# Masked attention on one Trainium2 core: the opening batch reordered, one tie dropped, four sums moved to VectorE

## The chip, the cores and the metric

The kernel runs on one core of a Trainium2 chip. The metric is device time in microseconds (us) of one execution. A core has the engines TensorE (PE in the profile; its weight loads are PEld), VectorE (DVE), ScalarE (ACT), GpSimd (POOL) and SyncE (SP); each works through its own queue of instructions in order, and engines wait for one another through semaphores. SP's queue issues most of the transfers (DMA), POOL's the gathers and scatters by index. Matrix products land in PSUM, a memory of eight banks of 512 float32 columns on 128 partitions; all else is in SBUF.

## The reference

Sixteen batches; each is a matrix x of 512 features by 1024 tokens with a mask of 0 and 1 over the tokens. Queries, keys and values are all the same projection.

```python
q = xt @ Wq.T                                   # xt: tokens by features, 1024 x 512
qh = q.reshape(B, T, NH, dk).transpose(0, 2, 1, 3)          # 8 heads of 64
scores = scale * jnp.einsum('bhqd,bhkd->bhqk', qh, qh)
logits = (scores * cmask + (1.0 - cmask) * NEG) * rmask
attn = jax.nn.softmax(logits, axis=-1)
ctx = jnp.einsum('bhqk,bhkd->bhqd', attn, qh)
out = ctx.transpose(0, 2, 1, 3).reshape(B, T, D) @ Wo.T
x = x + jnp.transpose(out, (0, 2, 1))
```

A masked key gets no weight. The row of a masked query has only equal logits, so it gets the plain mean over all tokens.

## The kernel before

Only tokens with mask 1 need attention: about half of 1024. For each batch the kernel gathers these (512 to 544 rows, `A`) and works on them alone; the masked tokens get one common row, made from the mean of x over all tokens. That mean needs the sum of every feature of x over 1024 tokens, which is read from a second copy of x, feature by feature: four transfers of 128x1024 (`load_all`, tile xm, two buffers) and four sums (`sum_half`, L459, on ScalarE). Batch 0 takes another way (`load_half`). Products are kept exact by splitting a float32 factor into two float16 parts, high and low, and summing three products.

The work of a batch b, and which lines do it:

- the gather (L422 on POOL) brings 128 rows of x at a time (tile xa; the rest in xt); the index comes from `index` (eight small matmuls L333, read by VectorE at L336)
- `xt` transposes each 128 rows on TensorE (L519, four matmuls into a tile pm); ScalarE writes the high part xh (L477), VectorE the low part xl (L478)
- `query(b, e, g)`: half g of the columns of feature chunk e, twelve matmuls (L548), copied by ScalarE (L552); after g=1 VectorE multiplies the edge (L555) and `qsplit` makes high and low parts (hl, L571 to L573), which four transfers of SP (L582 to L585) spread into xx, where the two heads of chunk e stand in forms of 128 and of 64 partitions
- `value(b, e)` turns the queries into rows (L608 for batch 0, L611 later; copied at L615) and sums squares of each row per head (sd, L594 or L598, then L599)
- `peaks`, `top`, `bottom` find for four heads the largest square, which bounds every score: `peaks` reduces on VectorE (smcol, L662 and L665), `top` transposes on TensorE (L671) and takes the maximum on VectorE (m, L674), `bottom` brings it to all partitions on TensorE (L681) and VectorE writes the exponentials' bias nm (L684 to L687)
- `scores(b, p, u)`: for head pair p and the query blocks 2u and 2u+1, eight or more matmuls (L774) into the tile pss, then four exponentials on ScalarE (L789) with their sums
- `attend(b, p)`: 16 products of exponentials and values (L809, each shown as two matmuls), copied by ScalarE (L832); `tail_scores` and `attend_tail` (L720, L827) for the columns past 512
- `recip_sums` and `recip_rows` invert the sums of the exponentials (L847 to L868, with a transpose L863 and two transfers), `norm` multiplies (L915 to L923), `project` multiplies with Wo (L933), adds x (L939) and scatters the rows (L1002)

pss has six banks. The scores of one call take banks 0 to 3, with A=544 a part of bank 4; the attention takes parts of banks 4 and 5; the start of bank 5 is the `spot` where index, `top` and `bottom` put their small results while the loop runs. Accesses of different engines to pss are ordered by the framework as one tile, and where they are in different banks the kernel lifts that order with `other_banks`. pm, the tile of all other products, has two buffers.

Every batch is a loop over 18 steps: head pair p by block i, with two steps in between that hold no block. Scores are made at steps 0, 3, 5, 7, 9, 12, 14 and 16; attention of a pair follows the first scores of the next. A dictionary `plan`, written out by hand, says for (step, half) what of the previous batch (o), of this one (b) and of the next one (n) stands where; half 0 comes after the step's scores and before its attention, half 1 after it. Batch 0 has a `plan` of its own. From batch 0 on TensorE's order is exactly that of the program (`manual_schedule`). The order on VectorE, ScalarE and the queues is made by a scheduler from priorities (`high_priority`) and due times.

`self.left` holds the exponentials of the last scores, `self.spot_reads` the reads of the spot. `self.exp` is the last exponential; `behind` asks the scheduler to put an instruction after others, `last_hl` is the latest copy of `qsplit`.

Of the kernel before, what the change touches and what calls it, by code (L numbers as in the profile page):

```python
# [15 lines left out]
ALU = mybir.AluOpType  # L16
AX = mybir.AxisListType
# [30 lines left out]
class Fast:  # L48
# [407 lines left out]
    def sum_half(self, b, k):  # L456
        s = self.st[b]
        with self.behind(*self.exp):
            self.nc.scalar.activation(s["xm"][k], s["xm"][k], AF.Copy, accum_out=s["ms2"][:, k:k + 1])  # L459

    def load_all(self, b, c, after=None):

        if c == 0:
            self.source(b)
        t = self.sb([P, T], F32, "xm", 2)
        src = self.x_nat[bass.ds(self.st[b]["row"], 1), c * P:(c + 1) * P, :].rearrange("o p t -> (o p) t")
        self.once(self.nc.sync.dma_start(out=t, in_=src), after)
        self.st[b]["xm"].append(t)
# [198 lines left out]
    def top(self, b, g):  # L667

        nc, s = self.nc, self.st[b]
        pt = self.spot(P)  # L670
        self.spotted(nc.tensor.transpose(pt, self.smcol[g], self.ident))  # L671
        m = s["m"] = self.sb([P, 1], F32, "m", 2)
        with self.tc.high_priority(offset=HPO):
            self.spot_reads += [nc.vector.tensor_reduce(m, pt, AX.X, ALU.max).ins] * self.spots  # L674

    def bottom(self, b, g):

# [64 lines left out]
    def scores(self, b, p, u):  # L742


        nc, s = self.nc, self.st[b]
        A = s["A"]
        if "z" not in s:
            s["z"] = self.sb([P, H, 4], F32, "z", 2)
            s["zt"] = self.sb([P, 2], F32, "zt", 2)
        xx = s["xx"][p]  # L750
        flat = self.ps.rearrange("p k n -> p (k n)")
        first = FIRST[A]
        places = [(k, 2 * u + i, first + (2 * k + i) * A) for k in range(2) for i in range(2)]
        last = []
        out = self.context_out

        calls, lanes = [], ([], [])
        for j, (k, i, at) in enumerate(places):
            rows = slice(i * P, (i + 1) * P)
            h = xx[k * DK:(k + 1) * DK, 3 * k, :]  # L760
            cuts = [at] + [c for c in (512 * (j + 1),) if at < c < at + A] + [at + A]
            for c0, c1 in zip(cuts, cuts[1:]):
                cols = slice(c0 - at, c1 - at)
                calls.append((c0, c1, xx[:, 2 * k, rows], xx[:, 2 * k + 1, cols]))
                if j == 1 and c0 == 1024:
                    calls.append((c0, c1, xx[:, 2 * k, rows], xx[:, 2 * k, cols]))
                else:
                    lanes[k].append((c0, c1, h[:, rows], h[:, cols]))
        for j in range(max(map(len, lanes))):
            calls += [l[j] for l in lanes if j < len(l)]  # L770
        banks = [c[0] // 512 for c in calls]
        for n, (c0, c1, w, x) in enumerate(calls):
            with self.behind(*last), self.tc.high_priority(offset=HPO if n else 0):
                m = nc.tensor.matmul(flat[:, c0:c1], lhsT=w, rhs=x, start=banks[n] not in banks[:n], stop=banks[n] not in banks[n + 1:])  # L774
            if out and banks[n] < 4:
                self.other_banks(m.ins, out)
            elif out and banks[n] not in banks[:n]:
                self.needs(m.ins, out)
            self.other_banks(m.ins, *self.spot_reads)
            if n == 0 and self.left:  # L780
                self.needs(m.ins, *self.left)
            last = [m.ins]
        self.beat = last[0]
        self.left, self.context_out = [], None
        ps = {}
        for j in (3, 0, 1, 2):
            k, i, at = places[j]
            t = self.sb([P, C], F32, "p", 12)[:, :A]
            e = nc.scalar.activation(t, flat[:, at:at + A], AF.Exp, bias=s["nm"][p // 2][:, p % 2 * 2 + k:p % 2 * 2 + k + 1],  # L789
                                     scale=SCALE, accum_out=s["z"][:, 2 * p + k, i:i + 1]).ins  # L790
            self.exp = [e]
            self.left.append(e)
            ps[k, i] = t
        s.setdefault("p", {}).setdefault(p, {}).update(ps)
# [250 lines left out]
    def run(self, flag):  # L1045
        B = self.B
        L = lambda f, *a: lambda: f(*a)
# [8 lines left out]
        def query(n, e, g):  # L1056
            u = [(1.37, L(self.query, n, e, g))]
            return u + [(0, L(self.qsplit, n, e))] if g else u

        def value(n, e):  # L1060
            return [(0.45, L(self.value, n, e))]
# [11 lines left out]
        for b in range(2, B):  # L1073
            n = 1 if b < B - 3 else 2 if b == B - 3 else 1 if b == B - 2 else len(queue)
# [96 lines left out]
        if True:  # L1171
            stack = ExitStack()
            for b in range(B + 1):
                o, n = b - 1, b + 1
# [6 lines left out]
                free, sums, rows, third, tail, rest = {}, [], [], [], [], []  # L1181
# [13 lines left out]
                pk, tp, bt = ((lambda o, g, f=f, c=c: [(c, L(f, o, g))]) for f, c in ((self.peaks, 0), (self.top, 0.1), (self.bottom, 0.1)))  # L1195
                new = [g for g in groups if b == g[0] - 2], [g for g in groups if b == g[0] - 1]
                if n < B:
                    q, x, v = (lambda e, g: query(n, e, g)), xt(n), (lambda e: [(0.25, L(self.value, n, e))])
                    tc, tv = ((lambda g, f=f, c=c: [(c, L(f, n, g))]) for f, c in ((self.tail_copy, 0), (self.value_tail, 0.25)))
                    rng = [(0, L(self.range_x, n, c)) for c in range(DC)]  # L1200
# [5 lines left out]
                    if b:  # L1206
                        pre = [(0, L(f, *g)) for g in new[0] for f in (self.permute, self.active)]
                        post = [(0.3, L(self.slots, *g)) for g in new[0]] + [(0, L(self.facts_sums, *g)) for g in new[1]]
                        end = [(0.1, L(self.facts_end, *g)) for g in new[1]]
                        plan = {(0, 0): sums + x[:2], (0, 1): x[2:4],  # L1210
                                (3, 0): rows + x[4:] + q(0, 0) + second, (3, 1): pre + q(0, 1) + carry, (4, 0): value(b, 3),
                                (5, 1): vt(b, 1) + pk(b, 1), (6, 0): post,
                                (7, 0): third + q(1, 0) + tp(b, 1), (7, 1): q(1, 1) + P_(0) + bt(b, 1), (8, 0): tc(0) + v(0) + end + rng[:2],
                                (10, 0): tv(0) + tail + q(2, 0), (11, 0): hot + rng[2:] + early,
                                (12, 0): q(2, 1), (12, 1): index + P_(1) + v(1), (13, 0): take[:3],
                                (14, 1): rest + pk(n, 0), (16, 0): P_(2) + take[3:], (16, 1): q(3, 0) + tp(n, 0) + q(3, 1),
                                (17, 0): bt(n, 0) + v(2) + tc(1) + [(0, L(self.means, n))]}
                        carry = P_(3)
                    else:
                        pre = [(0, L(f, *g)) for g in new[0] for f in (self.permute, self.active)]  # L1220
                        post = [(0.3, L(self.slots, *g)) for g in new[0]]
                        rng0 = [(0, apart(self.range_x, 0, c)) for c in range(DC)]
                        plan = {(0, 0): g1[4:] + query(0, 3, 0) + value(0, 2) + rng0,
                                (3, 0): query(0, 3, 1) + x[:1] + value(0, 3) + pk(b, 1), (4, 0): x[1:2],
                                (5, 0): x[2:3], (5, 1): x[3:],
                                (7, 0): tp(b, 1) + q(0, 0) + bt(b, 1) + q(0, 1), (8, 1): pre + q(1, 0),
                                (9, 1): post, (11, 0): hot + q(1, 1),
                                (12, 0): tc(0) + v(0) + rng[:2] + q(2, 0), (13, 1): index,
                                (14, 0): tv(0) + q(2, 1) + rng[2:] + take[:3], (14, 1): v(1) + q(3, 0) + pk(n, 0),
                                (16, 0): q(3, 1) + tp(n, 0) + take[3:], (16, 1): bt(n, 0),  # L1230
                                (17, 0): v(2) + tc(1) + [(0, L(self.means, n))]}
                else:
# [18 lines left out]
                for k, x in enumerate([x for x in (b + 2, self.extra.get(b + 2)) if x is not None and x < B]):  # L1251
                    if x > b + 2:
                        self.start(x)
                    elif b + 2 in self.extra.values():
                        continue
                    for c in range(DC):
                        at = 3 * c + k + (0 if b else 4)
                        free.setdefault(at, []).append(L(self.load_all, x, c, None if b else first_top))
                        free.setdefault(at + (2 if b + 2 in self.extra else 4), []).append(L(self.sum_half, x, c))
                def fill(st, half):  # L1260
                    for _, f in plan.get((st, half), []):
                        f()
# [175 lines left out]
```

## Time and profile before

| | |
|---|---|
| time, three runs | 974.54, 974.04, 973.05 us; median 974.04 |
| the profiled execution | 971.93 us, of which its span 970.2 us |
| granted TensorE clock, mean | 0.999 |
| chain of waits that ended last: share of PE, DVE, DMA, ACT | 80%, 7%, 5%, 3% |
| exponentials L789, 512 | 703 ns each, and 206 ns for reading their sum |
| scores L774, 1856 matmuls | 213.0 us |
| queries L548, three lines of 512 matmuls | 141.8, 141.1, 140.9 us |
| sums L459 of 128x1024, 60 | 1071 ns each |
| maximum L674, 32 | 290 ns each; VectorE idle before them 9.8 us for L789, 0.5 us for a product |
| transfers xm, 60 | 512 KB each |

Lines are those of the kernel before. An idle time is put down to the event that ended it. The span is that of the profiled execution; times of instructions are from its start. In the lists of work by order of time each line has the start, how long the group lasted, engine, line, operation, tiles and shape, the number of instructions, and in brackets how long the engine was idle before and for whom. Matmuls overlap: the list shows one of 512 columns as 0.38 us, while the next starts 0.22 us later.

### The profile page before, as it was taken

The numbers are of one execution on the slowest core, as the hardware profiler recorded it, in microseconds if no ns is written. First come the engines' busy times: TensorE is split into PE (matmuls) and PEld (weight loads), VectorE is DVE, ScalarE is ACT, GpSimd is POOL, SyncE is SP. The second block draws the span as 40 slices with busy tenths as digits, with TensorE's granted clock in tenths as the row PEclk, the third lists the DMA queues.
The fourth block names the chain that finished last, engine by engine and source line by source line (L and its number), as shares of the span: only waits on it lengthen the run. The fifth ranks groups of instructions, "written<-read, shape, count | busy, mean of one in ns | idle before, by whom it ended". The sixth has DMA issues, their size and how long they took to land.

```text
span 970.2 us, 22817 instructions
## 1 busy us (share of the span) xinstructions
PE 932.3 (96%) x8124; PEld 580.9 (60%) x8124; DVE 717.7 (74%) x2439; ACT 650.3 (67%) x1677; POOL 305.5 (31%) x309
## 2 busy tenths in 40 slices
PE   7788999999999999999999999999999999999997
PEld 4555666666666666666666566666666656565543
DVE  7768778777677767887688777877877778785664
ACT  5678857666777675776767678665767766565651
POOL 3101023043250522415144150422515135243452
PEclk9999999999999999999999999999999999999999
DMA  7656556466665676756657777654757757555552
GB/s 220 176 154 194 147 168 178 140 189 203 177 197 145 195 199 216 204 147 201 181 177 212 205 234 216 179 164 135 205 159 243 226 153 212 143 163 162 170 179 102
DMA packets 78568, 176.30 MB, mean 182 GB/s; under 512 B 14480, under 2 KB 22416, under 8 KB 78448
## 3 DMA queue, kind: packets, MB, share of 16 engines
q1 hardware_dynamic: 57392, 107.09, 39.2%
q0 software_dynamic: 21056, 67.68, 22.4%
q8 instruction: 66, 1.08, 0.5%
q14 instruction: 54, 0.44, 0.2%
HBM read 91.36 MB, written 33.91 MB: 129 GB/s over the span
## 4 chain that ended last, share of the span: by engine, by line
PE 80%; DVE 7%; DMA 5%; issue 3%; ACT 3%; SPq 1%; POOL 1%; POOLq 0%; DVEq 0%; ACTq 0%
PE pss L809 21%; PE pss L774 17%; PE pm L933 16%; PE pm L548 15%; PE pss L827 2%; PE pm L519 2%; DMA xm<-x_nat_in 2%; DMA xa<-x_in,idx 2%; PE pss L720 1%; PE pm L611 1%; ACT p L789 1%; DVE xl L478 1%; PE pss L933 1%; DVE xa L939 1%; DMA xx<-hl 1%
## 5 line engine op out<-in xcount | busy, mean ns | idle before, releaser
L789 ACT ACTIVATE p<-pss,nm 128x528 f32<-128x528 f32 (+2 forms) x512 | 354.5, 703 | 103.6 <-PE pss L774 101.5
L809 PE MATMUL pss<-p,v 128*64 128x264 f32 (+2 forms) x2048 | 242.4, 389 | 0.0
L774 PE MATMUL pss<-xx 128*128 128x118 f16 (+17 forms) x1856 | 213.0, 287 | 6.0 <-ACT p L789 3.8
L1002 POOL DMA_INDIRECT y_out<-xa,idx x68 | 81.8, 1203 | 409.5 <-DVE nq L686 98.3
L809 PEld LDWEIGHTS pss<-p,v 128*64 128x64 f32 x2048 | 141.4, 137 | 85.9 <-issue 4.8
L774 PEld LDWEIGHTS <-xx 128*128 128x128 f16 (+1 forms) x1856 | 103.2, 96 | 86.4 <-issue 34.3
L548 PE MATMUL pm<-xh,wqh 128*128 128x264 f16 (+5 forms) x512 | 141.8, 277 | 3.2 <-DVE xl L478 1.3
L548 PE MATMUL pm<-xh,wql 128*128 128x264 f16 (+5 forms) x512 | 141.1, 275 | 0.0
L548 PE MATMUL pm<-xl,wqh 128*128 128x264 f16 (+5 forms) x512 | 140.9, 275 | 0.0
L548 PEld LDWEIGHTS <-wqh 128*128 128x128 f16 x1024 | 96.4, 97 | 31.0 <-issue 11.9
L422 POOL DMA_INDIRECT xa<-x_in,idx x68 | 73.5, 1080 | 126.2 <-DMA y_out<-xa,idx 46.4
L789 ACT ACTIVATION_READ_ACCUMULATOR p<-pss,nm 128x1 f32 x512 | 105.4, 206 | 0.0
L933 PE MATMUL pm<-woh,ch 128*128 128x512 f16 x240 | 91.1, 380 | 0.0
L933 PE MATMUL pm<-woh,cl 128*128 128x512 f16 x240 | 90.9, 379 | 0.0
L933 PE MATMUL pm<-wol,ch 128*128 128x512 f16 x240 | 90.9, 379 | 0.0
L552 ACT ACTIVATE q<-pm 128x264 f32<-128x264 f32 (+5 forms) x128 | 51.0, 398 | 45.1 <-PE pm L548 44.9
L615 ACT COPY v<-pm 128x512 f32<-128x512 f32 x64 | 37.5, 587 | 57.9 <-PE pm L611 56.2
L939 DVE SCALAR_TENSOR_TENSOR xa<-pm,xa 128x512 f32<-128x512 f32 x61 | 41.7, 683 | 45.8 <-PE pm L933 45.3
L1002 POOL DMA_INDIRECT y_out<-xi,idx x60 | 64.1, 1068 | 34.3 <-PE pss L720 14.5
L933 PEld LDWEIGHTS <-ch 128*128 128x128 f16 x480 | 44.8, 98 | 47.5 <-issue 4.1
L422 POOL DMA_INDIRECT xi<-x_in,idx x60 | 59.9, 999 | 22.1 <-issue 15.8
L459 ACT ACTIVATE xm<-xm 128x1024 f32<-128x1024 f32 x60 | 64.1, 1071 | 2.0 <-DMA xm<-x_nat_in 1.9
(228 smaller groups left out, 1464.0 us busy)
## 6 DMA issues: line engine op xcount, KB each, us to landing
xm<-x_nat_in SPq DMA_DIRECT2D x60, 512.0 KB
xx<-hl SPq DMA_DIRECT2D x208, 136.0 KB
rb<-rd SPq DMA_DIRECT2D x72, 132.0 KB
xx<-hl SPq DMA_DIRECT2D x48, 128.0 KB
pt<-c SPq DMA_DIRECT2D x36, 132.0 KB
pt<-p SPq DMA_DIRECT2D x36, 132.0 KB
rb<-rd SPq DMA_DIRECT2D x32, 136.0 KB
ub<-ud SPq DMA_DIRECT2D x16, 256.0 KB
```

Of the source, the lines that this page charges most:

```text
L422: dma = self.nc.gpsimd.indirect_dma_start(out=tile[:n], out_offset=None, in_=self.x, in_offset=bass.IndirectOffsetOnAxis(ap=idx, axis=0))
L459: self.nc.scalar.activation(s["xm"][k], s["xm"][k], AF.Copy, accum_out=s["ms2"][:, k:k + 1])
L519: self.pe = nc.tensor.transpose(pt[:, c, :], x[:n, c * P:(c + 1) * P], self.ident[:n, :n]).ins
L548: self.beat = nc.tensor.matmul(pq, lhsT=w[:, c, e * P:(e + 1) * P], rhs=xx[:, c, cols], start=(k == 0), stop=(k == 3 * DC - 1)).ins
L552: nc.scalar.activation(s["q"][:, e, cols], pq, AF.Copy, scale=1.0 / (SX * SW))
L615: nc.scalar.copy(v, pv)
L774: m = nc.tensor.matmul(flat[:, c0:c1], lhsT=w, rhs=x, start=banks[n] not in banks[:n], stop=banks[n] not in banks[n + 1:])
L789: e = nc.scalar.activation(t, flat[:, at:at + A], AF.Exp, bias=s["nm"][p // 2][:, p % 2 * 2 + k:p % 2 * 2 + k + 1], scale=SCALE, accum_out ...
L809: mm = nc.tensor.matmul(pav[k * DK:(k + 1) * DK, g], lhsT=s["v"][p][:, i, k * DK:(k + 1) * DK], rhs=ps[k, i][:, cols], start=(i == 3), sto ...
L933: mm = nc.tensor.matmul(po[:cols.stop - cols.start], lhsT=a[:, e, cols], rhs=w[:, e, :], start=(e == 0 and k == 0), stop=(e == DC - 1 and ...
L939: return self.nc.vector.scalar_tensor_tensor(x, po, 1.0 / (SX * SW), x, ALU.mult, ALU.add).ins
L1002: dma = self.nc.gpsimd.indirect_dma_start(out=self.out, out_offset=bass.IndirectOffsetOnAxis(ap=idx, axis=0), in_=x, in_offset=None)
```

## The change

1. `top`: the maximum is told (`other_banks`) that it has nothing to do with the exponentials in `self.left`. The reading of `bottom`'s result (L684) keeps its order as it was.
2. `scores`: for the first call (batch 0, pair 0, blocks 0 and 1) the eight matmuls are sorted by head: the four that fill banks 0 and 1 first, then the four of banks 2 and 3; the four exponentials are issued in the order of the banks and not the last first.
3. The plan of batch 0: the transpose of chunk 1 of batch 1 moves from step 4 to step 5, behind that step's scores, beside chunk 2; query (2,1) of batch 1 moves from step 14, behind its scores, to step 13, behind `index`. `index` moves from the second half of step 13 to its first.
4. `sum_all`: the four sums of batch 1 become reductions on VectorE, put behind the latest `qsplit`. Batch 2's four sums, in the same stretch, stay on ScalarE; so do those of all later batches.

```diff
+    def sum_all(self, b, c, other):
+        s = self.st[b]
+        if not other:
+            return self.sum_half(b, c)
+        with self.behind(self.last_hl), self.nc.allow_low_precision(reason="float32"):
+            self.nc.vector.tensor_reduce(s["ms2"][:, c:c + 1], s["xm"][c], AX.X, ALU.add)
...
         with self.tc.high_priority(offset=HPO):
-            self.spot_reads += [nc.vector.tensor_reduce(m, pt, AX.X, ALU.max).ins] * self.spots
+            i = nc.vector.tensor_reduce(m, pt, AX.X, ALU.max).ins
+        if self.spots:
+            self.other_banks(i, *self.left)
+            self.spot_reads.append(i)
...
+        opening = b == 0 and p == 0 and u == 0
+        if opening:
+            calls.sort(key=lambda c: c[0] // (2 * A))
...
-        for j in (3, 0, 1, 2):
+        for j in (0, 1, 2, 3) if opening else (3, 0, 1, 2):
...
-                                (3, 0): query(0, 3, 1) + x[:1] + value(0, 3) + pk(b, 1), (4, 0): x[1:2],
-                                (5, 0): x[2:3], (5, 1): x[3:],
+                                (3, 0): query(0, 3, 1) + x[:1] + value(0, 3) + pk(b, 1),
+                                (5, 0): x[1:3], (5, 1): x[3:],
                                 (7, 0): tp(b, 1) + q(0, 0) + bt(b, 1) + q(0, 1), (8, 1): pre + q(1, 0),
                                 (9, 1): post, (11, 0): hot + q(1, 1),
-                                (12, 0): tc(0) + v(0) + rng[:2] + q(2, 0), (13, 1): index,
-                                (14, 0): tv(0) + q(2, 1) + rng[2:] + take[:3], (14, 1): v(1) + q(3, 0) + pk(n, 0),
+                                (12, 0): tc(0) + v(0) + rng[:2] + q(2, 0), (13, 0): index + q(2, 1),
+                                (14, 0): tv(0) + rng[2:] + take[:3], (14, 1): v(1) + q(3, 0) + pk(n, 0),
...
-                        free.setdefault(at + (2 if b + 2 in self.extra else 4), []).append(L(self.sum_half, x, c))
+                        free.setdefault(at + (2 if b + 2 in self.extra else 4), []).append(L(self.sum_all, x, c, b == 0 and x == 1))
```

In `plan`, `x` is `xt` of the next batch by chunks, `q(e, g)` its `query`, `v(e)` its `value`, `tp`, `bt` and `pk` are `top`, `bottom` and `peaks`, `tc` and `tv` the tail's copy and value, `take` the gathers of the batch after it, `hot`, `pre` and `post` the preparation of its index.

## The prediction

> **What bounds the kernel now.** I read the page's busy shares first, then the engines' busy time by stretches, then TensorE's and VectorE's work in order of time in the one stretch where TensorE is not full, and last the built programs' order of instructions and waits, which says what a wait is for but holds no time.
>
> ```profile
> PE 932.3 (96%) x8124; PEld 580.9 (60%) x8124; DVE 717.7 (74%) x2439; ACT 650.3 (67%) x1677; POOL 305.5 (31%) x309
> ```
>
> TensorE (PE) is the bound: only 970.2 - 932.3 = 37.9 us of the span are without a matmul. By stretches (us; then busy us and instructions of each engine, granted clock, DMA share, GB/s):
>
> ```profile
> 30.00:40.00 10.00, 6.47 (x45) 3.39 (x43) 7.92 (x26) 6.59 (x21) 2.78 (x3) 1.00 1.02 262
> 50.00:60.00 10.00, 7.04 (x55) 4.61 (x52) 5.52 (x22) 7.43 (x20) 0.00 (x0) 1.00 0.51 141
> 70.00:80.00 10.00, 8.25 (x80) 5.41 (x80) 9.19 (x35) 9.93 (x27) 1.89 (x2) 1.00 0.69 205
> 80.00:90.00 10.00, 7.88 (x77) 4.95 (x74) 8.39 (x32) 6.72 (x18) 2.77 (x3) 1.00 0.80 258
> 300.00:400.00 100.00, 98.93 (x896) 63.29 (x894) 73.68 (x243) 70.36 (x182) 35.34 (x34) 1.00 0.65 191
> ```
>
> The reader is to see that the holes lie in batch 0 (30 to 90 us), and that a later stretch is 99% full. Whatever batch 0 saves should therefore reach the end, and edits to other batches have next to nothing to win. TensorE's holes there, and the first line shown is the scores' wait for a transfer:
>
> ```profile
> 33.80 1.14 PE L774 MATMUL pss<-xx 128*128 128x512 f16 x6 [1.40 <-DMA xx<-hl]
> 38.59 1.57 PE L774 MATMUL pss<-xx 128*128 128x512 f16 x8 [1.79 <-ACT p L789]
> 44.04 0.66 PE L519 MATMUL pm<-ident,xa 128*128 128x128 f32 x4 [0.73 <-DVE xl L478]
> 52.29 0.33 PE L863 MATMUL pm<-ident,rcol 128*128 128x128 f32 x1 [1.05 <-DVE xl L478]
> 57.58 0.39 PE L681 MATMUL pss<-ident,m 128*128 128x4 f32 x2 [1.91 <-DVE m L674]
> 73.61 1.58 PE L774 MATMUL pss<-xx 128*128 128x512 f16 x8 [1.75 <-ACT p L789]
> 87.53 0.38 PE L681 MATMUL pss<-ident,m 128*128 128x4 f32 x2 [2.12 <-DVE m L674]
> ```
>
> Both holes at L681 name the maximum L674. VectorE (DVE) shows that they are different:
>
> ```profile
> 57.23 0.29 DVE L674 TENSOR_REDUCE m<-pss 128x1 f32<-128x128 f32 x1 [1.91 <-ACT p L789]
> 72.67 0.42 DVE L918 CAST ch<-c 128x512 f16<-128x512 f32 x1
> 77.74 0.33 DVE L555 TENSOR_TENSOR q<-q,hr 128x160 f32<-128x160 f32 x1 [0.60 <-ACT q L552]
> 80.97 0.24 DVE L534 TENSOR_SCALAR ms<-ms 128x4 f32<-128x4 f32 x2 [0.79 <-ACT xm L459]
> 81.93 0.69 DVE L598 TENSOR_TENSOR tmp<-v 128x512 f32<-128x512 f32 x1 [0.72 <-ACT v L615]
> 87.20 0.27 DVE L674 TENSOR_REDUCE m<-pss 128x1 f32<-128x128 f32 x1
> ```
>
> The first maximum stands idle for exponentials; the second is simply late in a queue that ran from 66.1 us with only 0.60 + 0.79 + 0.72 = 2.1 us of idleness.
>
> **Head by head.** Before, two matmuls of the first scores run before the hole of 1.40 us and six after; now four and four. In the built program the first of the four exponentials still holds their only wait for TensorE, and it is for the eighth matmul; so no exponential starts before the second head. What is saved is the shorter run after the transfer. A set of eight is four full matmuls 0.216 apart and four half-height ones (64 rows, two of each head): in the set at 38.59 us these start at 39.56 and the next query at 40.10, so 0.54 for four. Two of one head cost between half of that, 0.27, and all of it, 0.54, if it is only neighbours of different heads that overlap; at the pace of full ones 0.43. Gain 0 to 0.27, taken 0.1. It is the ScalarE (ACT) queue that passes it on, as the fourth exponential still stands behind L552 and L615.
>
> The Trainium skill, TensorEngine Tiling (Array Packing), section Tiling Modes, says that tiles on different rows of the array work independently and in parallel. By that rule the old interleaving bought overlap which the new order gives up, and the gain here is 0, the total 0.1 us smaller.
>
> **The moved transpose.** L519 of chunk 1 went into the hole at 44.04; now the scores come first, and they need the fourth exponential of the set before, which ended at 43.52 + 0.23 = 43.75. So they start near 43.8 less the 0.1, and three quarters of a microsecond earlier; but chunk 1 (0.6 us) then stands before the attention, which gains 0.73 - 0.6 = 0.1. L863 behind it (hole of 1.05) waits for xl of chunk 3, and that for L477 behind the sum L459 (49.35) and the copy L832 (50.38); those are earlier by about 0.15. Head and transpose together: 0.25 at L863, bounds 0 to 0.7.
>
> **The tie.** At L863 on, everything stands 0.25 earlier. The maximum now waits for its transpose alone: xl of chunk 4, one L485 (0.65), L868 (0.2), two L485 (1.3), so it starts at about 54.4 and ends at 54.7. TensorE is done with the query at 55.6 - 0.25. So L681 does not wait: 1.91 + 0.25 = 2.2 us gained here (bounds 1.9 to 2.6). The wait goes to L684, which reads the next small result of the same bank and is still tied to the exponentials; behind it on VectorE stand L847 and the norms' constants, nobody on TensorE until the scores of pair 2, whose exponentials come at about 60 against L687 at 57.5. In the other 15 batches the built order shows the wait for the exponentials on L847, one instruction later, so VectorE waits as before; TensorE lost 4.4 us on L681 in the whole span, 4.0 of them in batch 0. I cost that at 0, bounds -0.4 to +1.0 us: what is reordered there are small instructions around L555, whose 0.2 us is hidden under query and projection matmuls.
>
> **The moved query.** Index (0.35) and the query (2,1), 12 x 0.116 = 1.39 us, now stand where the hole of 1.75 was, ahead of the scores of step 14. The scores wait for the same exponential (73.55, now 71.35), and the query ends at about 71.1. The attention of pair 2, before at 76.88, comes after scores (1.50) and L637 (0.28): 73.2. Gain 3.7 so far; bounds 3.2 to 4.0. The attention also needs VectorE's idx (L336, same bank). The query's own L552 moves ahead of step 14's exponentials, 0.28 in their shadow; the gathers behind it on POOL's queue come earlier by the query's length too.
>
> **The sums.** Four sums of 128x1024 float32 leave ScalarE (1.07 + 0.2 us each, L459) for VectorE. No such reduction is in the trace. Twice L599 (128x512, 0.60 from start to start, 0.68 long) gives 1.2 to 1.36; less its fixed part, that of an instruction of four columns (0.08 to 0.16), 1.05 to 1.1. I take 1.14, the step of L324 (68.89 to 70.03), also 1024 columns. The first falls into VectorE's idle 3.25 us before 51.55, the second into its 3.21 before 66.10; both free. The third stands between L918 and L919, ahead of idx: L918 at 72.67 - 2.2 = 70.5, idx done at 70.5 + 0.33 + 1.14 + 0.61 + 0.14 = 72.7, 0.5 before the attention: hidden, but with this cover gone it is paid in full. Its load must have landed at 70.8; the load at 38.73 took 4.23, this one starts at about 62.3: landed near 67. SP's queue holds the next load and then the spread of the query (2,0) behind that sum's release. The fourth stands ahead of L534, and with it VectorE has no idleness left: adding L336 to L919 in the new order by start-to-start steps (0.14 to 0.65 each, the sum 1.14) gives 10.4 us, so smcol is ready at 72.6 + 10.4 = 83.0. TensorE could transpose it (L671) at 81.5 and waits 1.6; then L919 (0.61) and two L474 (0.2) before the maximum at 83.8, L681 at 84.1. Before: 87.53. **Gain at this point 3.4 us**: of the 3.7, 0.3 is given back, as TensorE now waits 2.3 for VectorE in two pieces where it waited 2.12. With each sum at 1.36 it is 3.0, at 1.05 3.6.
>
> Late next: nm of batch 1 (L687) stands behind L571 and L572 and gains only 89.05 - 86.8 = 2.2, its exponentials 2.6. The attention needs the first of them for its second half (at 89.0 against 87.8) and L720 the third (90.8 against 90.1): 0.7 us of cover, then paid one for one.
>
> **The sum.** 0.25 + 1.95 + 1.5 - 0.3 = 3.4 us. The profiled execution took 971.93 (span 970.2 and 1.7 around it) and would take 968.5; the three runs' median is 2.1 higher, 974.04, and becomes **970.6**.
>
> **Rivals.** *VectorE keeps up* (15%): its queue from 64 to 84 us is shorter than my steps say, because L605 to L672 wait for less. Then L671 goes at 81.5 and L681 at about 82.2, a gain of 5.3: 968.7. For: ScalarE no longer holds VectorE back at 77.7, 81.0, 81.9. Against: 2 x 1.14 fills just that. *It is eaten* (17%): a chain with less cover, idx before the attention (0.5) or the third exponential before L720 (0.7), is later by 1.5 to 3 us more than I add up; the gain is 0.4 to 1.9, 973. For: VectorE is at 9.19 of 10 there. Against: its steps are rows. *Slower* (10%): the third sum's load. VectorE in order waits at it, with L919, idx, and then the attention, the gathers and the spread of (2,1) behind. It decides from a landing at 70.8 + 0.5, and turns the sign at 71.3 + 3.4 = 74.7; a landing at 77.5, 15 us after its issue, gives 974.04 + 2.8 = 976.8. For: DMA is 63% to 80% busy here and the loads have two buffers, so each waits for the sum two before. Against: 4.23 us measured. *The change doesn't do what it says* is true of the head order (no early exponential) and in my sum already.
>
> **Numbers.** My forecast has 58%, its own range 969.4 to 971.8 (bounds above). Within 0.2%, 1.95 us, a measurement of this kernel can't be told from no change. Faster: 58 + 15 and a little of the eaten case: 0.75; same 0.15; slower 0.10. The range 967.8 to 973.2 leaves out the slower case and the ends of the two others.
>
> **What would show it.** TensorE: no idleness at the first L681 (near 55.4), under 0.5 us before step 14's scores, the attention of pair 2 near 73.2; L671 waiting for smcol near 83, the second L681 near 84.1. VectorE: sums of 1.05 to 1.36 us, the first two in idle time, the last two not. First exponentials still near 34.9. Later stretches as full as before. Wrong if a sum waits for its load, if idx ends after TensorE is ready for it, or if the 3.4 us at 84 us are not there at 200 us.

## The result, and the profile after

| | before | changed |
|---|---|---|
| median, range of the runs | 974.04 us (973.05 to 974.54) | 965.74 us (965.33 to 967.39) |
| ratio, 95% interval | | 0.9922 (0.9907 to 0.9936) |
| profiled execution, its span | 971.93 us, 970.2 us | 967.26 us, 965.6 us |

The kernel became 8.3 us faster. 970.6 had been forecast, a gain of 3.4: the sign was right, the size was not. Two numbers here need an explanation, and not one: the profiled executions lie only 4.7 us apart, the medians 8.3.

TensorE's line on the page, then the same stretches as before (us; then busy us and instructions of each engine, granted clock, DMA share, GB/s):

```profile
PE 933.0 (97%) x8124; PEld 581.2 (60%) x8124; DVE 721.3 (75%) x2443; ACT 645.2 (67%) x1669; POOL 305.1 (32%) x309
```

```profile
30.00:40.00 10.00, 7.09 (x45) 3.51 (x44) 7.11 (x26) 6.47 (x22) 2.78 (x3) 1.00 1.00 263
50.00:60.00 10.00, 8.93 (x69) 5.73 (x70) 7.21 (x28) 6.52 (x20) 0.00 (x0) 1.00 0.54 173
70.00:80.00 10.00, 9.68 (x80) 5.32 (x79) 10.00 (x34) 7.71 (x20) 3.83 (x3) 1.00 0.88 250
80.00:90.00 10.00, 9.25 (x97) 6.00 (x95) 9.84 (x38) 7.82 (x23) 1.90 (x3) 1.00 0.78 237
300.00:400.00 100.00, 98.94 (x885) 63.49 (x882) 77.76 (x250) 67.81 (x174) 36.11 (x34) 1.00 0.66 197
```

TensorE is idle for 965.6 - 933.0 = 32.6 us, 5.3 less than before, and the four stretches of ten in batch 0 hold just that much more work than they did (0.62 + 1.89 + 1.43 + 1.37 us); the stretch from 300 to 400 us is as full as it was. TensorE in order of time:

```profile
33.29 1.14 PE L787 MATMUL pss<-xx 128*128 128x512 f16 x4 [0.79 <-DMA xx<-hl]
43.29 1.57 PE L787 MATMUL pss<-xx 128*128 128x512 f16 x8 [0.50 <-ACT p L802]
51.51 0.33 PE L876 MATMUL pm<-ident,rcol 128*128 128x128 f32 x1 [1.07 <-DVE xl L485]
54.73 0.28 PE L691 MATMUL pss<-ident,m 128*128 128x4 f32 x2
70.65 1.57 PE L787 MATMUL pss<-xx 128*128 128x512 f16 x8 [0.32 <-ACT p L802]
72.52 3.67 PE L822 MATMUL pss<-p,v 128*64 128x256 f32 x32
80.89 0.33 PE L678 MATMUL pss<-ident,smcol 128*128 128x128 f32 x1
81.89 0.38 PE L691 MATMUL pss<-ident,m 128*128 128x4 f32 x2 [0.67 <-DVE m L681]
85.28 3.67 PE L822 MATMUL pss<-p,v 128*64 128x256 f32 x32
```

This execution was already 0.51 us early at its first scores (33.29 against 33.80), mostly because a gathered tile had landed earlier in the opening. Less these 0.51, the change has gained 2.34 us at the first L691, 3.85 at the attention of pair 2, 5.13 at the second L691 and 4.87 at the attention of pair 3 (85.28 against 90.66). From 140 to 560 us every matmul stands 5.21 us earlier, to within 0.02, which is 4.7; after that the distance goes up and down by up to 0.4 as waits for gathered tiles come and go. So the path became 4.7 us shorter, in batch 0 alone. VectorE before the second L691:

```profile
71.78 0.21 DVE L336 TENSOR_SCALAR idx<-pss,base 128x9 int32<-128x9 f32 x1
76.47 1.22 DVE L466 TENSOR_REDUCE ms<-xm 128x1 f32<-128x1024 f32 x1
80.68 0.15 DVE L672 TENSOR_TENSOR smcol<-smcol,sdt 128x4 f32<-128x4 f32 x1
81.55 0.28 DVE L681 TENSOR_REDUCE m<-pss 128x1 f32<-128x128 f32 x1
```

The maximum comes at 81.55 and not at 83.8, although VectorE is busy for all of 70 to 80 us.

### The profile page after: what moved, and what is told of

Same layout as the page of the kernel before. It is cut to its first block, busy times and chain, and to the rows that moved or that the text cites. A ratio compares the mean times of both kernels' runs of the same rounds, so it can differ in the third digit from the quotient of the medians.

```text
span 965.6 us, 22795 instructions
## 1 busy us (share of the span) xinstructions
PE 933.0 (97%) x8124; PEld 581.2 (60%) x8124; DVE 721.3 (75%) x2443; ACT 645.2 (67%) x1669; POOL 305.1 (32%) x309
## 3 DMA queue, kind: packets, MB, share of 16 engines
q8 instruction: 66, 1.08, 0.5%
## 4 chain that ended last, share of the span: by engine, by line
PE 78%; DVE 9%; ACT 5%; DMA 4%; issue 2%; SPq 1%; POOL 0%; POOLq 0%; DVEq 0%; ACTq 0%
PE pss L822 21%; PE pss L787 17%; PE pm L946 16%; PE pm L555 15%; ACT p L802 3%; PE pss L840 2%; PE pm L526 2%; PE pss L730 1%; DMA xx<-hl 1%; PE pm L618 1%; DVE xl L485 1%; PE pss L946 1%; DVE xa L952 1%; DMA xm<-x_nat_in 1%; DVE p L741 1%
## 5 line engine op out<-in xcount | busy, mean ns | idle before, releaser
L787 PE MATMUL pss<-xx 128*128 128x118 f16 (+17 forms) x1856 | 213.6, 287 | 5.1 <-ACT p L802 2.9
L787 PEld LDWEIGHTS <-xx 128*128 128x128 f16 (+1 forms) x1856 | 103.1, 96 | 86.8 <-issue 34.3
L555 PE MATMUL pm<-xh,wqh 128*128 128x264 f16 (+5 forms) x512 | 141.8, 277 | 3.3 <-DVE xl L485 1.3
L555 PE MATMUL pm<-xh,wql 128*128 128x264 f16 (+5 forms) x512 | 141.0, 275 | 0.0
L555 PE MATMUL pm<-xl,wqh 128*128 128x264 f16 (+5 forms) x512 | 140.9, 275 | 0.0
L555 PEld LDWEIGHTS <-wqh 128*128 128x128 f16 x1024 | 96.4, 97 | 31.4 <-issue 12.5
L946 PEld LDWEIGHTS <-ch 128*128 128x128 f16 x480 | 44.8, 98 | 47.5 <-issue 4.1
L845 ACT COPY c<-pss 128x528 f32<-128x528 f32 (+2 forms) x64 | 38.3, 598 | 37.8 <-PE pss L840 26.7
```

The source lines that it names most:

```text
L555: self.beat = nc.tensor.matmul(pq, lhsT=w[:, c, e * P:(e + 1) * P], rhs=xx[:, c, cols], start=(k == 0), stop=(k == 3 * DC - 1)).ins
L845: self.context_out = nc.scalar.copy(c[:, :A].rearrange("p (g c) -> p g c", g=2), pav).ins
L946: mm = nc.tensor.matmul(po[:cols.stop - cols.start], lhsT=a[:, e, cols], rhs=w[:, e, :], start=(e == 0 and k == 0), stop=(e == DC - 1 and ...
```

## The experiments

Two theories about the path were open (was the second hole at the maximum VectorE's queue or the tie's?), and two about the rest of the 8.3 us (waits elsewhere, or something that befalls single executions). Every run is compared with runs of the kernel before on the same chip. Each edit shifts the lines a little: L684, L688 and L691 are before's L681, L777, L781 and L787 its L774, and L681 in some kernels its maximum L674.

**Both kernels again, unchanged.**

> The kernel before once more, unchanged, for a second trace of it. Theory A (the change acts in batch 0 alone, by 4.9 us between 31 and 93 us, and the rest of the 8.3 us between the medians is where single executions fall): time 973.0 to 974.6 as before, and the matmuls between 31 and 93 us keep their distances to within 0.3 us (first L681 about 26.0 us after the first scores of batch 0, second L681 about 56.0); what differs from the first trace sits at the gathers (L519 waiting for xa) or behind the last matmul. Theory B (the change also gains some 3 us outside of batch 0, which the one profiled execution of before hides): the second trace shows waits in later batches or in batch 0 that the first trace does not have, at instructions that the change touches (L674, L681, L684, L847).

> The changed kernel once more, unchanged, for a second trace of it. Theory A: 965.3 to 967.4; the first scores of batch 0 to the second L691 take 50.8 us again, within 0.3, and if this execution is one of the shorter ones (965.3 to 965.8) the 1.8 us that it is shorter stand at the gathers, before 31 us or behind the last matmul. Theory B: the shorter executions have less idleness before L691, L694 or L840 to L876 in the later batches.

Before again: 973.40 us, ratio 0.9999 (0.9988 to 1.0009). The changed kernel: 965.33, ratio 0.9912 (0.9900 to 0.9925), so the gap is real. In its second trace the second L691 came 51.3 us after the first matmul of its scores, 0.5 later than expected; half of that was made up by the attention of pair 3, and at 400 us this trace is 4.6 us ahead of before, less what it had at 34 us, against 4.7 in the first. The matmuls of before kept their distances to within 0.1 us from the first scores to 87 us, and then this trace fell 1.59 us behind the first one by 91 us, with no wait. Neither theory had foreseen that. The granted clock shows it; here it is by the stretch in which it was low, and the stretch ahead of that:

```profile
84.00:87.41 3.41, 1.30 (x12) 0.90 (x9) 3.34 (x14) 3.02 (x10) 1.23 (x2) 1.00 0.93 322
87.41:90.82 3.41, 3.41 (x25) 2.06 (x26) 3.40 (x15) 0.80 (x2) 0.60 (x1) 0.50 0.92 287
```

TensorE ran at half its clock for 3.41 us, right behind a stretch of the same length in which it had been busy for 1.30 us only (the hole of 2.1 us before the second L681 and its surroundings). The first trace of before has no such fall while matmuls run; nor have the two of the changed kernel.

**The tie alone, the plan alone.** First the edit of `top` and then that of the plan, each made in the kernel before, as they stand in the change (of the plan's lines two pairs are shown, shortened):

```diff
-            self.spot_reads += [nc.vector.tensor_reduce(m, pt, AX.X, ALU.max).ins] * self.spots
+            i = nc.vector.tensor_reduce(m, pt, AX.X, ALU.max).ins
+        if self.spots:
+            self.other_banks(i, *self.left)
+            self.spot_reads.append(i)
```

```diff
-                                (5, 0): x[2:3], (5, 1): x[3:],
+                                (5, 0): x[1:3], (5, 1): x[3:],
...
-                                (14, 0): tv(0) + q(2, 1) + rng[2:] + take[:3],
+                                (14, 0): tv(0) + rng[2:] + take[:3],
```

> The kernel before with only the tie dropped. Theory A: TensorE's idleness before the first L691 of batch 0 (1.91 us) goes, all after it moves by 1.9 us, and 1.5 to 1.9 of it are left at 93 us and at the end: about 972.1. Theory B (the tie costs in the other 15 batches too): 0.4 to 1.5 us more come between 93 us and the end, below 971.5. A rival to both: the wait moves on to the norms of pair 2 and VectorE's queue takes the gain back at the second L691: 973.5 to 974.1.

> The kernel before with only the moved transpose and the moved query. Theory A with the sums as the enabling part: the attention of pair 2 starts 3.6 to 4.0 us earlier (near 73.1 against 76.88), but ScalarE keeps its sums (93% to 99% busy at 66 to 81 us) and hands q, xm and v to VectorE hardly earlier, so that the second L681 moves by only 0.2 to 1.5 us: 972.5 to 973.8. The rival, that VectorE has the room and ScalarE does not hold it: the second L681 moves by 3 us or more: 971 or less.

The tie alone: 968.51 us, 0.9948 (0.9935 to 0.9961), far more than any theory gave it. The plan alone: 970.67, 0.9977 (0.9963 to 0.9991), also more than I had expected. Its path is nearer to the expectation: the second L681 came 1.58 us earlier, less the start, against 0.2 to 1.5. The 3.6 to 4.0 us expected at the attention of pair 2 were a miss: 1.65 us were measured, as the tie's part of them is not in this run. TensorE in order of time, first the kernel with the tie dropped:

```profile
55.34 0.28 PE L684 MATMUL pss<-ident,m 128*128 128x4 f32 x2
71.26 1.58 PE L777 MATMUL pss<-xx 128*128 128x512 f16 x8 [1.74 <-ACT p L792]
83.80 0.39 PE L684 MATMUL pss<-ident,m 128*128 128x4 f32 x2 [0.74 <-DVE m L674]
```

and the one with the plan moved:

```profile
57.77 0.39 PE L681 MATMUL pss<-ident,m 128*128 128x4 f32 x2 [1.91 <-DVE m L674]
73.80 1.57 PE L774 MATMUL pss<-xx 128*128 128x512 f16 x8 [0.33 <-ACT p L789]
86.39 0.38 PE L681 MATMUL pss<-ident,m 128*128 128x4 f32 x2 [2.11 <-DVE m L674]
```

Dropping the tie closes the first hole and takes the second from 2.12 to 0.74: the second L684 stands 3.73 us earlier (3.56 without what this execution had at its first scores), not 1.9. The plan closes the hole at step 14 (1.4 us) and leaves both holes at the maximum as they were. At 400 us, and without what each execution had at its first scores, the tie alone is 3.0 us ahead of before and the plan alone 1.6; the changed kernel's 4.7 is their sum, to within 0.1.

**The sums, on either side, and the head order.** The edit of the sums, taken out of the changed kernel in the first run and put into the kernel before in the second, and that of the head order, put into the kernel before (only what changes in each line):

```diff
-L(self.sum_half, x, c)
+L(self.sum_all, x, c, b == 0 and x == 1)
...
+        if opening:
+            calls.sort(key=lambda c: c[0] // (2 * A))
...
-        for j in (3, 0, 1, 2):
+        for j in (0, 1, 2, 3) if opening else (3, 0, 1, 2):
```

> The changed kernel with its four sums back on ScalarE. If the sums are what lets VectorE keep up (on ScalarE they hold VectorE back by 2.1 us at L562, L541 and L605 before the second maximum): L678 waits, the second L691 comes 1 to 2 us later than in the changed kernel (50.8 us after the first scores there), and the time is 966.5 to 967.5. If the tie and the moved query account for all of the gain and the sums only trade one queue for the other: 965.0 to 966.2, with the second L691 within 0.4 us of the changed kernel's.

> The kernel before with only the four sums moved to VectorE. My prediction's view (two of them lengthen a full VectorE queue by 1.14 us each, against 2.1 us of waits for ScalarE that go): the second L681 within 0.5 us of before's, time 972.5 to 973.7. If VectorE has the room and ScalarE held it: the second L681 1 to 2 us earlier and the hole before it as much shorter, 971 to 972. If the sums cost their length: 1 to 2 us later, 974.5 or more.

> The kernel before with only the first scores put head by head. The first exponential of batch 0 still waits for the eighth matmul, and the run after the transfer (1.08 us in before) takes 1.0 to 1.1: no gain. Against that: if the first two exponentials start with the first head, the first of them starts 0.5 us earlier against the end of the transfer.

The changed kernel with its sums on ScalarE: 965.69 us, ratio 0.9925 (0.9907 to 0.9944), its matmuls 0.39 us behind the changed kernel's at 34 us and 0.47 at 560, second L684 at 82.13 after a wait of 0.59. The kernel before with the sums on VectorE: 972.34, ratio 0.9998 (0.9985 to 1.0011). Its holes:

```profile
57.68 0.38 PE L688 MATMUL pss<-ident,m 128*128 128x4 f32 x2 [1.90 <-DVE m L681]
89.30 0.57 PE L688 MATMUL pss<-ident,m 128*128 128x4 f32 x2 [2.12 <-DVE m L681]
```

So the sums gain and cost nothing: on ScalarE they leave VectorE 1.59 us of idleness before L598, on VectorE they fill that. And the second hole is 2.12 us with the sums and without them, with the query moved and not. That speaks against a queue. What is constant is another distance: in all eight traces of this study from kernels that have the tie, the second maximum starts 1.08 us (1.25 in one, below) behind the start of the fourth exponential of step 16, the first one 0.83 behind its own. Here are the exponential and the maximum in the kernel before, and then in the changed one:

```profile
86.12 0.70 ACT L789 ACTIVATE p<-pss,nm 128x512 f32<-128x512 f32 x1
```

```profile
86.64 0.64 DVE L571 CAST hl<-q 128x544 f16<-128x544 f32 x1
87.20 0.27 DVE L674 TENSOR_REDUCE m<-pss 128x1 f32<-128x128 f32 x1
```

```profile
81.76 0.70 ACT L802 ACTIVATE p<-pss,nm 128x512 f32<-128x512 f32 x1
```

```profile
81.41 0.24 DVE L481 CAST xh<-ms 128x4 f16<-128x4 f32 x2
81.55 0.28 DVE L681 TENSOR_REDUCE m<-pss 128x1 f32<-128x128 f32 x1
```

With the tie the maximum had also been ordered behind L555, L560 and L571, the work on a query that ScalarE copies only between the third and the fourth exponential. Without it, it stands behind the cast of the means and starts ahead of that exponential. No idle time shows on VectorE before the tied maximum, as L571 runs until then. The distance alone does not settle it, since L555 itself waits for ScalarE's copy just ahead of the fourth exponential; what settles it is that the tie by itself takes the second hole from 2.12 to 0.74 us when it is dropped and from 0.67 to 2.08 when it is put back (below), while the query, the sums and the head order leave it at 2.1. Nor is the whole second hole the tie's: in the six traces without it 0.54 to 0.74 us are left, and there VectorE is at other work until the maximum starts.

The head order alone, in one execution: first exponential 1.18 us behind the first score after the transfer, as before (34.98 - 33.80); no gain. Its execution of 974.18 us is a long one for another reason. Six stretches of it, each of 3.41 us:

```profile
55.13:58.54 3.41, 1.50 (x13) 1.06 (x12) 1.24 (x10) 3.25 (x9) 0.00 (x0) 1.00 0.35 129
58.54:61.96 3.42, 3.42 (x18) 2.26 (x16) 1.84 (x11) 0.61 (x2) 0.00 (x0) 0.50 0.60 204
72.20:75.61 3.41, 1.66 (x21) 1.30 (x19) 3.41 (x12) 3.41 (x12) 0.00 (x0) 1.00 0.49 158
75.61:79.03 3.42, 3.42 (x26) 1.91 (x26) 3.18 (x14) 3.42 (x10) 0.00 (x0) 1.00 0.93 191
85.85:89.26 3.41, 1.38 (x12) 0.95 (x10) 3.34 (x14) 3.18 (x10) 1.07 (x2) 1.00 0.96 320
89.26:92.68 3.42, 3.34 (x25) 2.07 (x26) 3.37 (x16) 0.80 (x2) 0.74 (x1) 0.50 0.92 305
```

1.50 and 1.38 us of work in 3.41 are followed by half the clock, 1.66 is not. Against the first trace of before the matmuls lose 1.67 us in the one fall and 1.53 in the other; the trace of the sums on VectorE has the same two, 1.66 and 1.59.

**The holes filled.** If the clock falls for want of work, useless work must make the kernel faster. The edit, in front of the waiting instructions (here the two maxima; with four holes it stands also in `scores`, in the same form):

```diff
-        m = s["m"]
+        m = s["m"]; (b, g) in [(0, 1), (1, 0)] and filler(self, 5)
...
+def filler(self, n):
+    t = self.pm([P, 4, P])
+    for _ in range(n):
+        self.nc.tensor.matmul(t, lhsT=self.on16, rhs=self.on16.unsqueeze(1).broadcast_to([P, 4, P]), start=True, stop=True)
```

> The kernel before with 20 matmuls of ones added (4 x 5, 128x512, some 1.1 us each time) in front of four instructions of batch 0 at which TensorE waits 1.75 to 2.1 us: the second scores of pair 0, the two L681 and the scores of step 14. Nothing else changes, on any engine, and no wait gets shorter. Theory clock (holes of about 2 us make the granted clock fall to one half for 3.41 us in some executions, and this is what the median of before pays beyond its path): the median falls from 973.1 to 970.5 to 971.5, no execution is above 972.5, the mean granted clock of each run is 0.998 or more; the profiled execution shows the same waits, less 1.1 us each, at the same places. Theory path (the spread of before comes from transfers or from waits that the change touches): the median stays at 972.5 to 974 and the spread stays, or the time grows.

> The kernel before with 10 matmuls of ones (2 x 5) in front of the two L681 of batch 0 alone, a second try at what the clock costs apart from the path. Theory clock: no stretch of 3.41 us that ends with these holes is under 0.45 busy any more, the profiled execution has no fall of the clock at 55 to 65 or 84 to 95 us, and in 10 of 12 runs the granted clock is 0.998 or more (before: under half of the runs); mean time 0.7 to 1.5 us under before's mean of the same call. Theory path: mean within 0.4 us of before's or above, although the clock is higher.

Four holes filled: 971.90 us against 971.98, 0.9994 (0.9981 to 1.0008). The granted clock rose (0.998 or more in 10 of 12 runs, in 11 of 23 of before's), if not in every run as expected, but the median did not fall and the slowest run took 975.25: a miss for the time. At the same granted clock of 0.999 the filled kernel took 971.7 us (mean of 6 runs) and before 970.7 (4 runs), though in its trace the matmuls keep before's distances to within 0.1 us from the first scores to 560 us; where it lost this stays open. Two holes filled, at the maxima only: 971.12 us against 973.26, 0.9986 (0.9972 to 1.0000), clock 0.998 or more in 10 of 12 runs against 5 of 23, mean time 971.5 (standard error 0.5) against 973.1 (0.3). Ten matmuls more, and 1.6 us less, although one run, at a clock of 0.996, took 976.51. The stretches that hold its holes, and the next ones:

```profile
56.04:59.45 3.41, 2.58 (x20) 1.78 (x19) 1.63 (x13) 2.43 (x9) 0.00 (x0) 1.00 0.39 89
59.45:62.87 3.42, 3.42 (x27) 1.92 (x27) 2.97 (x10) 1.42 (x5) 0.00 (x0) 1.00 0.42 150
83.34:86.76 3.42, 3.06 (x22) 1.69 (x18) 3.35 (x14) 3.01 (x10) 1.35 (x2) 1.00 0.86 271
86.76:90.17 3.41, 2.73 (x32) 1.94 (x33) 3.41 (x15) 1.67 (x5) 1.04 (x2) 1.00 0.89 290
```

The clock moved in both kernels, the time in one only, and there the interval reaches 1: that useless work can pay is likely, and not shown.

**Each part undone.** The diffs are the reverse of those shown; the third run has the first two of them in the kernel before and nothing else.

> The changed kernel with the tie put back. Theory tie (both holes at the maximum are the tie's: in every run so far that has the tie the maximum starts 0.83 and 1.08 us after the start of the fourth exponential before it, whatever VectorE's queue holds): the holes before the two L681 of batch 0 are 1.9 and 2.1 us again, the second maximum starts 1.08 us after its fourth exponential, and 3.2 to 3.8 us of the path gained are lost; time 969 to 970.5, with runs of a granted clock below 0.998 again. Theory queue (the second hole was VectorE's queue, which the sums relieve): the second hole is 0.6 to 1.2 us, the loss 1.9 to 2.4 us, 967.5 to 968.5.

> The changed kernel with the query and the transpose back in their old places. Both theories: the hole before the scores of step 14 is 1.7 us again instead of 0.3, 1.4 us are lost there and some 0.1 to 0.3 at the transpose: 966.8 to 968. With the hole back one stretch of 3.41 us is at 0.45 to 0.5 busy, so the granted clock may fall in a few runs.

> The kernel before with the tie dropped and the query and the transpose moved, without the head order and the sums. If these two edits are all that counts: 965.0 to 966.2, the matmul stream from the first scores to the end within 0.4 us of the changed kernel's. If the head order or the sums gain anything: 966.5 or more.

With the tie back: 971.65 us, 0.9978 (0.9966 to 0.9989), longer than expected.

```profile
56.93 0.50 PE L688 MATMUL pss<-ident,m 128*128 128x4 f32 x2 [1.90 <-DVE m L681]
85.32 0.33 PE L678 MATMUL pss<-ident,smcol 128*128 128x128 f32 x1 [0.41 <-DVE smcol L672]
87.31 0.39 PE L688 MATMUL pss<-ident,m 128*128 128x4 f32 x2 [1.67 <-DVE m L681]
```

Both holes are back, 1.90 and 0.41 + 1.67 = 2.08 us, as the tie's theory said and not VectorE's queue. At the second L688 this trace is 5.42 us behind the changed kernel's; 0.1 of these it had at the first scores and some 1.65 came at 57 to 60 us, where its clock halved, so the tie costs 3.7 us there. Its maximum came 1.25 us behind the fourth exponential, 0.17 more than elsewhere: a full queue adds something, but little. 10 of its 12 runs had a granted clock under 0.998. With the plan back: 967.95, 0.9946 (0.9931 to 0.9962), as expected, and the hole of 1.74 us before step 14. Tie and plan alone: 965.33, 0.9919 (0.9903 to 0.9935), the matmuls 0.60 us behind the changed kernel's at 34 us and 0.48 at 400. These two edits are the whole gain.

## Why the prediction was right in sign and wrong in size

By its own steps (the gains have 0.51 us taken off for the early start):

| step | forecast | measured |
|---|---|---|
| head by head | 0.1 us | 0: the run after the transfer took 1.07 us against 1.08 |
| head and transpose at L863 | 0.25 | 0.27 |
| first L681, all | 2.2 | 2.34 |
| attention of pair 2 | 3.7 | 3.85 |
| a sum on VectorE | 1.14 | 1.12 to 1.14 from start to start |
| idx done | 72.7 | 71.9 (72.4 without the early start); no wait |
| smcol ready, second L681 | 83.0, 84.1 | 80.8, 81.9 (81.3 and 82.4 without the early start) |
| gain there | 3.4 | 5.13 |
| gain left at 400 us | 3.4 | 4.7 |
| other 15 batches | 0 | 0, and up to 0.4 either way at gathered tiles |

*Head by head.* In the changed kernel's trace the half-height matmuls of the first set after the transfer start at 33.83 and 34.05, one after the other; before, two started at 34.34 and two at 34.56 and 34.57, in pairs. Two alone take as long as two pairs. The Trainium skill, TensorEngine Tiling (Array Packing), section Tiling Modes, has tiles on different rows of the array work in parallel; the traces agree.

**The reading that failed** is the sentence "the second is simply late in a queue that ran from 66.1 us". Most of the second hole was the tie's, like the first: some 1.4 of its 2.12 us. I had looked for idleness on VectorE ahead of the maximum, saw none, and called it a queue; but an ordering that the tie made had filled the place with other work. The sum was not wrong by this, as it went by the new order, in which the maximum stands right behind L919 and L474: from smcol to the second L681 it had 1.1 us (83.0 to 84.1), and 1.1 were measured (80.8 to 81.9). What it had wrong by this is where the gain comes from: the tie alone gains 3.0 us at 400 us and not 1.95.

**The step of the sum that failed first** is the time of VectorE's queue, 10.4 us from L336 to L919, which took 9.0. With that, the 1.6 us that L671 was to wait for smcol became some 0.1 (L678 at 80.89), and "of the 3.7, 0.3 is given back" turned into a further gain of 1.3. About 1.1 of the 1.4 comes from steps read in before's order: where an instruction's result is read by its neighbour, the neighbour starts later. In before, L918 takes 0.46 us to the start of L919, which reads it (84.62 to 85.08), but 0.33 to that of an unrelated one (72.67 to 73.00); L598 of 256 columns 0.46, and 0.29 in the changed order, where another instruction stands between. The rival *VectorE keeps up* had the right size (5.3) and a queue shorter than the steps said, as it was, but the wrong reason: it let the sums free ScalarE, and they did nothing.

*What was late next.* The bias of batch 1 (nm) was to gain only 2.2, with 0.7 of cover behind it; it gained 3.9 (84.60 against 89.05) and little was lost behind it: 5.13 became 4.7.

**The second, and the larger,** is the sum's last line, which took the 2.1 us between the profiled execution and the median as a constant and carried them over. The path makes only 1.3 of the 4.9 us between 970.6 and 965.74; the other 3.6 stand in this line. Those 2.1 us are not constant. Over 80 runs of before, in three series on three chips, the time follows the mean granted clock: 974.4 us at 0.995 (19 runs), 972.7 at 0.997 (28), 970.9 at 0.999 (8); 0.84 us for each 0.001 within a series. The mean is 972.9 at 0.9967; ten runs of the changed kernel have 965.9 at 0.9986, none below 0.998. At 0.999 the kernels are 970.9 - 965.5 = 5.4 us apart, 0.7 more than the path in the traces; the other 1.6 of the 7.0 is the clock. The profiled execution of before happened to have none of these falls. The 7.0 is itself rough: in the one series that has both kernels, on one chip, the means are 7.8 apart. What the first comparison shows beyond 7.0, and the 0.7, stay open: gathered tiles after 560 us alone move a trace of one and the same kernel by up to 1.9 us (two traces of before: 1.41 us behind at 560, 0.49 ahead at 955), and no run was made to hold them still.

That the clock falls are mostly the tie's follows from where they stand. In 14 traces TensorE was busy for 38% to 44% of a stretch of batch 0 in seven cases, all of them the holes of 1.9 to 2.1 us before the maxima in kernels with the tie; each was followed by half the clock. In 15 other stretches of batch 0 it was busy for 47.5% to 53%, the holes of 1.75 us before scores among them, and none was followed by a fall. Which of these shares an execution meets depends on where the stretches begin, and that differs from one execution to the next: around the second hole a stretch began at 83.76 us in the first trace of before and was 48% full, and at 84.00 in the second and was 38% full. The tie need not be the only cause. The two kernels that lack it but keep the hole of 1.74 us before step 14 have one run of 5 and one of 6 at a clock of 0.996, of which there is no trace; in the 21 runs of the three kernels with both edits none is below 0.998.

The Trainium skill, TensorE: Matmul & The Clock Gate, section "Part 1: The HAM clock gate", has a free-running window of 3413 ns behind the gate; the falls here, 3.41 us long and at places that vary, agree. The section "HAM oscillation" of that page of the Trainium skill advises against idle gaps over some 3.4 us; here gaps of 1.9 to 2.1 us were enough, and the measurement decides.

## What to carry to other kernels

A wait that a tie causes can hide as a full queue: compare the distance from the suspected releaser over several executions or variants. A constant distance speaks for a tie and against a queue, whose length varies; taking the tie out by itself decides. Read start-to-start steps from pairs that stand in the new order, not the old. And before a median is compared with a profiled execution, look at the mean granted clock of the runs: a hole of 2 us in a full TensorE can cost its own length and, in some executions, 1.5 to 1.7 us more. Even useless matmuls may pay there, which one of the two filled kernels here suggests.

## What was not expected of the hardware

- Half the clock for 3.41 us after a stretch of 3.41 us with TensorE busy 38% to 44%, in all of seven cases in batch 0, and after one of 41% at the end of the changed kernel; none in fifteen from 47.5% to 53%. What lies between was not met.
- With ten useless matmuls added the kernel took 1.6 us less in the mean (0.9986, 0.9972 to 1.0000); with twenty it took as long as without (0.9994).
- A VectorE instruction starts about 0.12 us later if it reads the result of the one before it (behind L918 after 0.46 us against 0.33, behind L916 after 0.38 against 0.26).
- A VectorE sum of 128x1024 float32 took 1.20 to 1.22 us, ScalarE's 1.07 and 0.2 for reading the sum.
